# Router logits of the first twelve batches on VectorE instead of TensorE, in a fused four-layer attention and MoE kernel

## The chip, the cores and the metric

One Trainium2 chip; the kernel runs on one core of it. The metric is device microseconds for one launch, from the core's first to its last instruction and what the runtime adds around it.

## The reference

Sixteen batches of 256 tokens of width 256, float32. Four residual layers follow each other, and the last is a routed mixture of experts:

```python
x = x + L0_xattn(ctx_1024, layernorm(x))      # 8 heads of 128, keys: 256 context + 256 own rows
x = x + L0_ffn(layernorm(x))                  # 256 -> 1024 -> 256, weights changed per batch by 16 tokens
x = x + L1_xattn(layernorm(x), ctx, ctx)      # one head of width 256
x = x + L1_ffn(layernorm(x))
# L1_ffn: E = 8 experts of width 256
inh = sigmoid(x @ Wr / temperature)           # the logits: x is (256, 256) a batch, Wr is (256, 8)
w = ...                                       # weights from |inh - 1/e|, a zone, a fallback to the best two
out = sum_e w[:, e] * ((silu(x @ Wg[e]) * (x @ Wu[e])) @ Wd[e])
```

The change touches how `x @ Wr` is computed, when its results are used, and the code for rows beyond the usual capacity.

## The kernel before

The work is a stream of 128 heads (16 batches of 8) of the first attention. The outer loop `for n in range(NS + 2)` writes out one head after another: scores `sc` and their maxima `nm` (`s1`), the exponentials on ScalarE, scaling of the rows on GpSimd (`s1_scale`), 32 by 32 transposes on VectorE and a hop through DRAM to finish the transposition (`s2`, `s2_fetch`: `tb`, `hop`, `pT`), and two heads later the product with the values (`s3`: `po`, `outT`). `s0q` and `s0k` project the next head's queries and keys; their results `qT` and `kT` are moved by ScalarE or VectorE (`evict`).

Between these steps `gap` gives TensorE other work. It holds a list of jobs, generators that write out some instructions and then yield how long, in planned TensorE time (`Clock.pe`), they want to wait. The order of every engine's queue is thereby fixed when the program is built; each engine runs its queue in order and waits on semaphores. One job per batch is `chain`, everything after the first attention: the output projection `px`, the first feed-forward layer (`W1e`, `ph`, `gelu`, `W2e`, `pf`), the second attention (`pv1`, `pq1`, `sc1`, `po1`), and the logits. A second job, `route`, waits until the chain is done and turns logits into weights and slots; then GpSimd scatters the batch's rows with 16 indirect DMAs into `slots_d` (line 811), from where the experts read them. Chain b starts when head 2 of batch b + 1 is written. Jobs talk through sets: `A.fed` (the first layer of the feed-forward is written), `A.fed_forward`, `A.weighed` (the routing has read the logits).

The logits of a batch, before: the normalized rows `row` (lines 613 to 615) are transposed in 32 by 32 blocks by VectorE (`to_blocks`, line 306, tile `yd_b`), written to DRAM and fetched back as `ydT` (`from_blocks`, line 317; five DMAs on SyncE's queue), copied into order (lines 918 and 922), and multiplied by `Wr_sb` on TensorE (`pl`, four products of 128 by 8 each, eight passes). This holds for batches 0 to 13 (`hopped`); batches 14 and 15 transpose on TensorE (`turned_tile`, tile `ydT_p`).

Tiles shared in turn matter here: `W1e` holds the batch's changed first-layer weights (8 KB a partition), `pT1` the second attention's probabilities. `ev` is a row set broadcast to all partitions from DRAM (line 410), 512 KB an issue; `behind_fetch` is a list of such issues, one of which is put out per head, behind the fetch of `pT`.

The experts (`experts`, class `G`) start from head 124 on, and run on after the last head; each group of up to 512 rows is loaded, transposed through DRAM (`hop_rows_b`, `yTd`) and multiplied (`pg`, `pu`, `pd`); its results are added into the output by indirect DMAs of GpSimd (line 1324). Rows beyond the planned capacity are worked in units (class `U`); those beyond `AMONG` lie behind a branch that the device takes only if a count on the device asks for it.

Of the kernel before, what the change touches and what calls it, by code (L numbers as in the profile page):

```python
# [12 lines left out]
F32 = mybir.dt.float32  # L13
# [3 lines left out]
ALU = mybir.AluOpType  # L17
# [12 lines left out]
def xattn_ffn_kernel(  # L30
# [220 lines left out]
    WvT = keep.tile([P, DC, D], F32, name="WvT")  # L251
    Wr_sb = keep.tile([P, DC, E], F32, name="Wr_sb")

# [93 lines left out]
    def chain(b, A, behind):  # L347
# [16 lines left out]
        def raw_tile(tag, name):  # L364
            return wk.tile([P, QP, DC, TC, QB], F32, tag=tag, name=name)
# [65 lines left out]
        while behind is not None and b - 1 not in A.fed_forward:  # L431
            yield 0.4


        od = wk.tile([P, DC, 2 * NI], F32, tag="od", name=f"od_{b}")
        nc.vector.tensor_scalar(
# [84 lines left out]

        rs = ln_rstd(mv, "q")
        yield queued - 0.3
        while behind is not None and not behind.done:
            yield 0.4
        y = wk.tile([P, TC, D], F32, tag="y", name=f"yc_{b}")
        ln_apply(y, x_b, mv, rs)
# [54 lines left out]
        if hopped:  # L582
            hop = to_blocks(wk, pr, TC, "tbc", 2, f"pr1_{b}_b")
            yield SENT
            raw = raw_tile("raw_c", f"pr1T_{b}")
            from_blocks(raw, hop)
            yield LANDED + 3.0
            pT = wk.tile([P, TC, S], F32, tag="pT1", bufs=1, name=f"pT1_{b}")
            for m in range(TC):
                evict(pT[:, m, :], in_order(raw)[:, m], None, None)  # L590
            yield 4.0
        else:
            pT = turned_tile(pr, "pT1", f"pT1_{b}")
            yield 2.5
        mv = mv_tile("d")
        for c in range(TC):
            ri = small.tile([P, 1], F32, tag="ri1", name=f"ri1_{b}_{c}")
            nc.vector.reciprocal(ri, sums[c])
            po = mm_tile(D, f"po1_{b}_{c}")
            for m in range(TC):  # L600
                mm(po, pT[:, m, ts(c, P)], v1[:, m, :], start=(m == 0), stop=(m == TC - 1))
            nc.vector.scalar_tensor_tensor(
                x_b[:, c, :], po, ri, x_b[:, c, :], ALU.mult, ALU.add
            )
            stats(c, "d", mv)


        rs = ln_rstd(mv, "d")
# [4 lines left out]
        row = A.row[b] = wk.tile([P, TC, ROW], F32, tag="row", bufs=2, name=f"row_{b}")  # L613
        ln_apply(row[:, :, 0:D], x_b, mv, rs)
        nc.vector.tensor_copy(row[:, :, D + E], number[:, b * TC : (b + 1) * TC])
        if hopped:
            hop = to_blocks(wk, row, TC, "tbc", 2, f"yd_{b}_b")
            yield SENT
            raw = raw_tile("raw_c", f"ydT_{b}")
            from_blocks(raw, hop)  # L620
            yield LANDED
            ydT = wk.tile([P, DC, S], F32, tag="q1T", name=f"ydT_{b}")
            for d in range(DC):
                evict(ydT[:, d, :], in_order(raw)[:, d], None, None)
            yield 4.0
        else:
            yield 1.4
            ydT = turned_tile(row, "q1T", f"ydT_{b}")
            yield 1.6
        while b >= 1 and b - 1 not in A.weighed:  # L630
            yield 0.4
        pl = mm_tile(TC * E, f"pl_{b}")
        for c in range(TC):
            for d in range(DC):
                mm(
                    pl[:, ts(c, E)], ydT[:, d, ts(c, P)], Wr_sb[:, d, :],
                    start=(d == 0), stop=(d == DC - 1),
                )
        A.z[b] = wk.tile([P, TC, E], F32, tag="z", name=f"z_{b}")
        nc.vector.tensor_scalar(  # L640
            A.z[b].rearrange("p t e -> p (t e)"), pl, lasting["invt"], None, ALU.mult
        )


    class Plan:
# [177 lines left out]
    class A:  # L823
        xs, ctxT, outT, cin, kvT, v = {}, {}, {}, {}, {}, {}
        row, z = {}, {}
        projected, fed, fed_forward, weighed = set(), set(), set(), set()
        tails = {}


# [1 line left out]
    with ExitStack() as sh, ExitStack() as sa, ExitStack() as sf:  # L831
# [290 lines left out]
        def load_late(h):  # L1122
            if h == 0:
                nats["W2"] = load_turn(W2, DC, HC, "W2e")
            if h == 1:
                nats["Wv"] = load_turn(Wv_w, DC, DC, "v1")
                nats["qk"] = load_fold()
            if h == 5:
                nc.sync.dma_start(Wo_sb, Wo.rearrange("(h p) d -> p h d", p=P))
                nc.sync.dma_start(Wr_sb, Wr.rearrange("(c p) e -> p c e", p=P))  # L1130
                lasting["b2"] = row_everywhere(b2, "b2_bc")
                lasting["bv1"] = row_everywhere(Wv_b, "bv1_bc")
                lasting["scale"] = row_everywhere(ffn_scale, "scale_bc")
                lasting["invt"] = row_everywhere(temperature, "temp_bc")
            if h == 7:
                nc.vector.reciprocal(lasting["invt"], lasting["invt"])

        def all_turns():
# [206 lines left out]
        class U:  # L1345


            def __init__(self, part, j):
                self.part, self.j = part, j
                self.u = sum(UNITS[:part]) + j  # L1350
                self.name = f"{part}_u{j}"

            def place(self):
                return nc.values_load(
                    Plan.starts[0:1, self.u : self.u + 1], engines=(mybir.EngineType.SP,),
                    min_val=0, max_val=E * NTOKS[self.part] - P,
                )

            def expert(self):
                return nc.values_load(  # L1360
                    Plan.who[0:1, self.u : self.u + 1], engines=(mybir.EngineType.PE,),
                    min_val=0, max_val=E - 1,
                )

            def weight(self, to):
                by = D_.more.tile([P, E], F32, tag="by_u", bufs=2, name=f"by_{self.name}")
                nc.vector.tensor_tensor(by, self.rows[:, D : D + E], Plan.weigh[:, self.u], ALU.mult)
                nc.vector.tensor_reduce(to, by, AX.X, ALU.add)

            def load(self):  # L1370
                tag = ("y", "yT")[self.u % 2]
                rows = wk.tile(
                    [P, ROW], F32, tag=tag, bufs=1, name=f"rows_{self.name}",
                    padded_shape=[P, DC * S],
                )
                self.rows = rows
                nc.sync.dma_start(rows, slots_d[self.part][bass.ds(self.place(), P), :])
# [37 lines left out]
            def down(self):  # L1415
# [188 lines left out]
        some = nc.values_load(beyond[0:1, 0:1], min_val=0, max_val=1)  # L1604
        all_slots = nc.values_load(beyond[0:1, 1:2], min_val=0, max_val=1)
        with tc.If(some > 0):
            for part in range(2):
                for j in range(AMONG[part], UNITS[part]):
                    u = U(part, j)
                    u.load()  # L1610
                    u.turn()
                    u.gates()
                    u.turn_h()
                    u.down()

            with tc.If(all_slots > 0):
                for part in range(2):
# [48 lines left out]
```

## Time and profile before

| | |
|---|---|
| median of 3 runs | 1810.41 us (1808.53 to 1811.94) |
| the profiled execution's own time | 1815.16 us, its span 1813.4 us |
| TensorE (PE) busy | 1780.6 us, 98% |
| VectorE (DVE) busy | 1196.6 us, 66% |
| ScalarE (ACT) busy | 586.0 us, 32% |
| GpSimd (POOL) busy | 830.9 us, 46% |
| DMA | 325.01 MB, 179 GB/s on average |
| granted TensorE clock | 0.995 |

How to read it: a line of a group gives source line, engine, operation, the tiles written and read, the shape, the count, then the busy time, the mean duration of one, and the idle time of the engine just before, with what ended it. A line of a timeline gives the start in us from the span's start, the duration, the engine and the instruction; in brackets the engine's idle time ahead of it and what ended that. Matmuls are pipelined, so their durations overlap, and the distance between starts is what one costs. L80 is the helper that issues every matmul; tiles tell them apart. SPq is SyncE's DMA queue.

### The profile page before, as it was taken

To read this page: it belongs to the slowest core of one execution; us is meant where nothing else is said; L and a number is where in the kernel's file an instruction comes from. 1 tells how busy PE (TensorE), PEld (TensorE's weight loads), DVE (VectorE), ACT (ScalarE), POOL (GpSimd) and SP (SyncE) were. 2 spreads that over 40 slices of the span, in tenths; PEclk is the share of its full clock that TensorE was granted. 3 is DMA by queue.
4 is the path that set the end of the run, shared out by engine and by line. 5 is a ranking of instruction groups with operands and counts; after the bars stand their busy time and mean duration, and the time that the engine had idled before them with its cause. 6 is when DMAs were issued, how large, how long until landed. Compare 5 with 4: busy or idle time off the path is not lost.

```text
span 1813.4 us, 22509 instructions
## 1 busy us (share of the span) xinstructions
PE 1780.6 (98%) x6508; PEld 1206.7 (67%) x6508; DVE 1196.6 (66%) x3332; ACT 586.0 (32%) x1306; POOL 830.9 (46%) x979
## 2 busy tenths in 40 slices
PE   8999999999999999999999999999999999999987
PEld 4566666666666666666666666666666677666655
DVE  4465676767676767676767676767666667675544
ACT  3433434343434343333333333333333311211100
POOL 2122224444435353535353535353534357776765
PEclk9999999999999999999999999999999999999999
DMA  6653546565655555555556555555545668899986
GB/s 215 184 185 117 174 139 190 167 189 168 187 169 188 168 184 172 184 172 178 173 181 174 180 177 177 179 178 175 181 156 157 197 161 216 227 234 235 200 168 112
DMA packets 264746, 325.01 MB, mean 179 GB/s; under 512 B 32893, under 2 KB 217385, under 8 KB 264617
## 3 DMA queue, kind: packets, MB, share of 16 engines
q1 hardware_dynamic: 235720, 273.67, 49.9%
q0 software_dynamic: 28848, 49.83, 11.7%
q8 instruction: 54, 0.88, 0.2%
q14 instruction: 76, 0.61, 0.1%
q10 hardware_dynamic: 48, 0.01, 0.0%
HBM read 161.91 MB, written 161.48 MB: 178 GB/s over the span
## 4 chain that ended last, share of the span: by engine, by line
PE 92%; DMA 2%; DVE 2%; SPq 1%; issue 1%; POOL 1%; ACT 0%; POOLq 0%; DVEq 0%; ACTq 0%
PE po L80 13%; PE sc L80 13%; PE pv L80 13%; PE pk L80 11%; PE pq L80 7%; PE px L80 6%; PE ph L80 6%; PE pf L80 6%; PE pg L80 5%; PE pu L80 5%; PE pd L80 5%; DMA yTd<-hop_rows_b 1%; PE pl L80 1%; SPq L317 1%; DMA pT<-hop 0%
## 5 line engine op out<-in xcount | busy, mean ns | idle before, releaser
L987 ACT ACTIVATE pr<-sc,nm 128x512 f32<-128x512 f32 x256 | 173.7, 683 | 479.7 <-DVE nm L981 418.4
L995 POOL TENSOR_SCALAR pr<-pr,ri 128x512 f32<-128x512 f32 x256 | 179.0, 709 | 322.7 <-DVE ri L994 317.8
L811 POOL DMA_INDIRECT slots_d<-row,at_slot x256 | 253.2, 989 | 70.4 <-issue 70.4
L80 PE MATMUL po<-pT,v 128*128 128x256 f32 x1024 | 242.3, 379 | 2.6 <-DVE W2T L1048 1.5
L80 PE MATMUL sc<-kT,qT 128*128 128x512 f32 x512 | 241.0, 593 | 1.5 <-ACT kT L920 1.5
L80 PE MATMUL pk<-kvT,Wk_sb 128*128 128x512 f32 x512 | 241.3, 594 | 0.0
L80 PEld LDWEIGHTS po<-pT,v 128*128 128x128 f32 x1024 | 193.8, 190 | 70.8 <-issue 38.1
L80 PE MATMUL pv<-Wv_sb,kvT 128*128 128x512 f32 x512 | 235.0, 592 | 0.0
L1033 DVE TENSOR_SCALAR outT<-po,cvec 128x256 f32<-128x256 f32 x128 | 61.2, 478 | 246.0 <-PE po L80 230.1
L1003 DVE STREAM_TRANSPOSE tb<-pr 128x512 f32<-128x512 f32 x256 | 165.9, 686 | 13.2 <-DMA hop<-tb 11.7
L80 PEld LDWEIGHTS pv<-Wv_sb,kvT 128*128 128x128 f32 x512 | 97.0, 190 | 108.2 <-issue 103.1
L981 DVE TENSOR_REDUCE nm<-sc 128x1 f32<-128x512 f32 x256 | 160.3, 663 | 2.0 <-PE sc L80 1.9
L80 PEld LDWEIGHTS sc<-kT,qT 128*128 128x128 f32 x512 | 96.9, 190 | 69.9 <-issue 61.2
L80 PEld LDWEIGHTS pk<-kvT,Wk_sb 128*128 128x128 f32 x512 | 97.7, 191 | 68.4 <-issue 61.6
L80 PE MATMUL pq<-kvT,Wq_sb 128*128 128x256 f32 x512 | 133.5, 383 | 0.0
L80 PEld LDWEIGHTS pq<-kvT,Wq_sb 128*128 128x128 f32 x512 | 96.7, 191 | 41.8 <-issue 28.2
L80 PE MATMUL px<-Wo_sb,outT 128*128 128x256 f32 x512 | 121.8, 381 | 0.0
L80 PE MATMUL ph<-ybT,W1e 128*128 128x256 f32 x512 | 121.0, 379 | 0.0
L1324 POOL DMA_INDIRECT out_dram<-o,at x65 | 102.3, 1574 | 36.3 <-issue 19.2
L452 POOL TENSOR_TENSOR W2e<-ev,od 128x256 f32<-128x256 f32 x120 | 78.5, 681 | 88.0 <-DMA ev<-ev_d 88.0
L918 ACT COPY v<-pv 128x512 f32<-128x512 f32 (+1 forms) x132 | 70.8, 536 | 148.1 <-PE pv L80 146.7
L80 PE MATMUL pf<-W2e,hT 128*128 128x256 f32 x512 | 118.0, 379 | 0.0
(259 smaller groups left out, 2695.4 us busy)
## 6 DMA issues: line engine op xcount, KB each, us to landing
hop<-tb SPq DMA_DIRECT2D x128, 512.0 KB
pT<-hop SPq DMA_DIRECT2D x512, 128.0 KB
ev<-ev_d SPq DMA_DIRECT2D x32, 512.0 KB
rows<-slots_d SPq DMA_DIRECT2D x14, 530.0 KB
hop_rows_b<-rows_b SPq DMA_DIRECT2D x13, 512.0 KB
yTd<-hop_rows_b SPq DMA_DIRECT2D x52, 128.0 KB
rows<-slots_d SPq DMA_DIRECT2D x15, 397.5 KB
hop_rows_b<-rows_b SPq DMA_DIRECT2D x14, 384.0 KB
```

Source lines behind the costliest of these rows:

```text
L80: nc.tensor.matmul(out, lhsT, rhs, **kw)
L317: nc.sync.dma_start(dst[ts(m, QB)].rearrange("r a d c s -> r a (d c s)"), from_[m])
L452: (nc.gpsimd if b < B - 1 else nc.vector).tensor_tensor(W2e[:, c, d, :].rearrange("p (i a) -> p i a", i=NI), evs[1][:, :, c * NA : (c + 1) ...
L811: ins = nc.gpsimd.indirect_dma_start(out=slots_d[part], out_offset=bass.IndirectOffsetOnAxis(ap=at_slot[:, c, e : e + 1], axis=0), in_=row ...
L918: nc.scalar.copy(out, src)
L981: nc.vector.tensor_reduce(nm, sc, AX.X, ALU.max, negate=True)
L987: nc.scalar.activation(pr, sc, AF.Exp, bias=nm, accum_out=sm)
L995: nc.gpsimd.tensor_scalar(pr, pr, ri, 1.0, ALU.mult, ALU.mult)
L1003: nc.vector.transpose(tb[:, :, c, :], heads[n][c][0].rearrange("p (m f) -> p m f", m=QP))
L1033: nc.vector.tensor_scalar(o, po, col("bv", h), None, ALU.add)
L1324: ins = nc.gpsimd.indirect_dma_start(out=out_rows[0 : sum(NTOKS[: self.part + 1]), :], out_offset=bass.IndirectOffsetOnAxis(ap=self.at[:, ...
```

## The change

For batches 0 to 11 the logits are computed on VectorE. `Wr` is transposed once at the start and stored in DRAM (`WrT_d`). For each such batch two DMAs broadcast it to all partitions, four experts each (512 KB), into the tile `W1e`, after the next batch's `ph` is written; then 16 `tensor_tensor_reduce` operations, one for each expert and each 128 rows, multiply a row tile by one expert's vector and sum along the row. They are spaced by 1.4 of planned time. The transposes, the hop and the products `pl` of these batches are gone. Batches 12 to 15 take the path of TensorE's transposes, which before only 14 and 15 took.

The waits between jobs follow: the next chain's `W1e` waits until the logits two batches back are written (`A.scored`), its use of `pT1` until those one batch back are, and its second attention waits for the previous second attention (`A.attended`) rather than the whole previous chain. Routing of a batch still waits for its chain and so comes later.

The units of the first part that lie behind the branch become a loop on the device (class `W`).

```diff
@@ -251,6 +251,10 @@
     WvT = keep.tile([P, DC, D], F32, name="WvT")
     Wr_sb = keep.tile([P, DC, E], F32, name="Wr_sb")
+    WrT_d = dram.tile([E, D], F32, tag="WrT_d", bufs=1, name="WrT_d")
+    zero = keep.tile([P, 1], F32, name="zero")
+    nc.gpsimd.memset(zero, 0.0)
+
@@ -429,6 +433,9 @@
             yield 0.2
         yield max(landed[0], there) - Clock.pe
         while behind is not None and b - 1 not in A.fed_forward:
+            yield 0.4
+
+        while b >= 2 and b - 2 not in A.scored:
             yield 0.4
@@ -521,7 +528,7 @@
         rs = ln_rstd(mv, "q")
         yield queued - 0.3
-        while behind is not None and not behind.done:
+        while behind is not None and b - 1 not in A.attended:
             yield 0.4
         y = wk.tile([P, TC, D], F32, tag="y", name=f"yc_{b}")
         ln_apply(y, x_b, mv, rs)
@@ -585,6 +592,8 @@
             raw = raw_tile("raw_c", f"pr1T_{b}")
             from_blocks(raw, hop)
             yield LANDED + 3.0
+            while behind is not None and b - 1 not in A.scored:
+                yield 0.4
             pT = wk.tile([P, TC, S], F32, tag="pT1", bufs=1, name=f"pT1_{b}")
             for m in range(TC):
                 evict(pT[:, m, :], in_order(raw)[:, m], None, None)
@@ -603,6 +612,7 @@
                 x_b[:, c, :], po, ri, x_b[:, c, :], ALU.mult, ALU.add
             )
             stats(c, "d", mv)
+        A.attended.add(b)
         rs = ln_rstd(mv, "d")
@@ -613,33 +623,60 @@
         row = A.row[b] = wk.tile([P, TC, ROW], F32, tag="row", bufs=2, name=f"row_{b}")
         ln_apply(row[:, :, 0:D], x_b, mv, rs)
         nc.vector.tensor_copy(row[:, :, D + E], number[:, b * TC : (b + 1) * TC])
-        if hopped:
-            hop = to_blocks(wk, row, TC, "tbc", 2, f"yd_{b}_b")
-            yield SENT
-            raw = raw_tile("raw_c", f"ydT_{b}")
-            from_blocks(raw, hop)
-            yield LANDED
-            ydT = wk.tile([P, DC, S], F32, tag="q1T", name=f"ydT_{b}")
-            for d in range(DC):
-                evict(ydT[:, d, :], in_order(raw)[:, d], None, None)
-            yield 4.0
+        if b < B - 4:
+
+
+            while b + 1 not in A.fed:
+                yield 0.4
+
+            yield 12.0
+            Wr_all = wk.tile([P, E, D], F32, tag="W1e", name=f"Wr_all_{b}")
+            landed = []
+
+            def wr_everywhere(half):
+                nc.sync.dma_start(
+                    Wr_all[:, ts(half, E // 2), :].rearrange("p e d -> p (e d)"),
+                    WrT_d[ts(half, E // 2)].rearrange("e d -> (e d)").partition_broadcast(P),
+                )
+                landed.append(Clock.pe + 8.0)
+
+            behind_fetch.extend([lambda: wr_everywhere(0), lambda: wr_everywhere(1)])
+            while b >= 1 and b - 1 not in A.weighed:
+                yield 0.4
+            z = A.z[b] = wk.tile([P, TC, E], F32, tag="z", name=f"z_{b}")
+            part_of = wk.tile([P, D], F32, tag="pT1", name=f"zy_{b}", padded_shape=[P, TC * S])
+            for e in range(E):
+                if e % (E // 2) == 0:
+                    half = e // (E // 2)
+                    while len(landed) <= half:
+                        yield 0.2
+                    yield landed[half] - Clock.pe
+                for c in range(TC):
+                    nc.vector.tensor_tensor_reduce(
+                        out=part_of, in0=row[:, c, 0:D], in1=Wr_all[:, e, :], op0=ALU.mult,
+                        op1=ALU.add, scale=1.0, scalar=zero, accum_out=z[:, c, e : e + 1],
+                    )
+                    yield 1.4
+            z = z.rearrange("p t e -> p (t e)")
+            nc.vector.tensor_scalar(z, z, lasting["invt"], None, ALU.mult)
         else:
             yield 1.4
             ydT = turned_tile(row, "q1T", f"ydT_{b}")
             yield 1.6
-        while b >= 1 and b - 1 not in A.weighed:
-            yield 0.4
-        pl = mm_tile(TC * E, f"pl_{b}")
-        for c in range(TC):
-            for d in range(DC):
-                mm(
-                    pl[:, ts(c, E)], ydT[:, d, ts(c, P)], Wr_sb[:, d, :],
-                    start=(d == 0), stop=(d == DC - 1),
-                )
-        A.z[b] = wk.tile([P, TC, E], F32, tag="z", name=f"z_{b}")
-        nc.vector.tensor_scalar(
-            A.z[b].rearrange("p t e -> p (t e)"), pl, lasting["invt"], None, ALU.mult
-        )
+            while b >= 1 and b - 1 not in A.weighed:
+                yield 0.4
+            pl = mm_tile(TC * E, f"pl_{b}")
+            for c in range(TC):
+                for d in range(DC):
+                    mm(
+                        pl[:, ts(c, E)], ydT[:, d, ts(c, P)], Wr_sb[:, d, :],
+                        start=(d == 0), stop=(d == DC - 1),
+                    )
+            A.z[b] = wk.tile([P, TC, E], F32, tag="z", name=f"z_{b}")
+            nc.vector.tensor_scalar(
+                A.z[b].rearrange("p t e -> p (t e)"), pl, lasting["invt"], None, ALU.mult
+            )
+        A.scored.add(b)
     class Plan:
@@ -823,7 +860,8 @@
     class A:
         xs, ctxT, outT, cin, kvT, v = {}, {}, {}, {}, {}, {}
         row, z = {}, {}
-        projected, fed, fed_forward, weighed = set(), set(), set(), set()
+        projected, fed, fed_forward, attended = set(), set(), set(), set()
+        scored, weighed = set(), set()
         tails = {}
@@ -1133,6 +1171,14 @@
                 lasting["scale"] = row_everywhere(ffn_scale, "scale_bc")
                 lasting["invt"] = row_everywhere(temperature, "temp_bc")
             if h == 7:
+                tp = tr_tile("WrT_p")
+                for d in range(DC):
+                    turned(tp[0:E, d, :], Wr_sb[:, d, :], ident)
+                WrT = wk.tile(
+                    [E, D], F32, tag="pT1", bufs=1, name="WrT", padded_shape=[E, TC * S]
+                )
+                nc.vector.tensor_copy(WrT, tp[0:E, 0:DC, :].rearrange("p d s -> p (d s)"))
+                nc.sync.dma_start(WrT_d, WrT)
                 nc.vector.reciprocal(lasting["invt"], lasting["invt"])
         def all_turns():
@@ -1347,30 +1393,34 @@
             def __init__(self, part, j):
                 self.part, self.j = part, j
-                self.u = sum(UNITS[:part]) + j
+                u = self.u = sum(UNITS[:part]) + j
+                self.of = slice(u, u + 1)
+                self.tag = ("y", "yT")[u % 2]
                 self.name = f"{part}_u{j}"
             def place(self):
...
@@ -1429,11 +1479,21 @@
                 )
                 apart(ins, f"out_{self.name}", others(self.part))
+        class W(U):
+
+
+            def __init__(self, j):
+                self.part, self.u = 0, j
+                self.name = "0_w"
+                self.of = bass.ds(j, 1)
+
+            tag = "y"
+
         class V(U):
             def __init__(self, part, e, t, j):
-                self.part, self.u = part, j
+                self.part, self.tag = part, ("y", "yT")[j]
                 self.e, self.t = e, t
                 self.name = f"{part}_v{j}"
@@ -1604,14 +1664,13 @@
         some = nc.values_load(beyond[0:1, 0:1], min_val=0, max_val=1)
         all_slots = nc.values_load(beyond[0:1, 1:2], min_val=0, max_val=1)
         with tc.If(some > 0):
-            for part in range(2):
-                for j in range(AMONG[part], UNITS[part]):
-                    u = U(part, j)
-                    u.load()
-                    u.turn()
-                    u.gates()
-                    u.turn_h()
-                    u.down()
+            with tc.For_i(AMONG[0], UNITS[0]) as j:
+                u = W(j)
+                u.load()
+                u.turn()
+                u.gates()
+                u.turn_h()
+                u.down()
             with tc.If(all_slots > 0):
                 for part in range(2):
```

More of the change, by code (lines that the diff above doesn't have):

```diff
@@ L1354, in place @@
                 return nc.values_load(
-                    Plan.starts[0:1, self.u : self.u + 1], engines=(mybir.EngineType.SP,),
+                    Plan.starts[0:1, self.of], engines=(mybir.EngineType.SP,),
                     min_val=0, max_val=E * NTOKS[self.part] - P,
@@ L1360, in expert @@
                 return nc.values_load(
-                    Plan.who[0:1, self.u : self.u + 1], engines=(mybir.EngineType.PE,),
+                    Plan.who[0:1, self.of], engines=(mybir.EngineType.PE,),
                     min_val=0, max_val=E - 1,
@@ L1366, in weight @@
                 by = D_.more.tile([P, E], F32, tag="by_u", bufs=2, name=f"by_{self.name}")
-                nc.vector.tensor_tensor(by, self.rows[:, D : D + E], Plan.weigh[:, self.u], ALU.mult)
+                nc.vector.tensor_tensor(
+                    by, self.rows[:, D : D + E],
+                    Plan.weigh[:, self.of].rearrange("p u e -> p (u e)"), ALU.mult,
+                )
                 nc.vector.tensor_reduce(to, by, AX.X, ALU.add)
             def load(self):
-                tag = ("y", "yT")[self.u % 2]
                 rows = wk.tile(
-                    [P, ROW], F32, tag=tag, bufs=1, name=f"rows_{self.name}",
+                    [P, ROW], F32, tag=self.tag, bufs=1, name=f"rows_{self.name}",
                     padded_shape=[P, DC * S],
```

## The prediction

> **What bounds the kernel now.** I read the page first (shares of each engine), then the table of stretches, then what TensorE (PE) waits for, and last the order of time around the operations that the change removes.
>
> From the page and from the stretches (length, busy time of PE, PEld, DVE, ACT, POOL, granted clock, DMA share, GB/s):
>
> ```profile
> PE 1780.6 (98%) x6508; PEld 1206.7 (67%) x6508; DVE 1196.6 (66%) x3332; ACT 586.0 (32%) x1306; POOL 830.9 (46%) x979
> ...
> 340.00:1330.00 990.00, 989.16 (x3615) 675.91 (x3614) 693.98 (x1944) 363.05 (x822) 443.91 (x576) 1.00 0.57 177
> ...
> 1600.00:1700.00 100.00, 99.05 (x345) 64.32 (x344) 60.47 (x162) 16.42 (x33) 66.93 (x49) 1.00 0.97 246
> ```
>
> In the steady part PE is idle 0.84 us of 990. Two equal pieces of the chain of waits (pf at 902.94 and 993.82) give a batch of 90.9 us, so that stretch is 10.9 batches, and VectorE (DVE) works 693.98 / 10.9 = 63.7 us of each: 27 us are free. The time is PE's sum; another engine counts only where it makes PE wait. In the last 300 us the DMA engines are nearly full as well.
>
> PE's own waits, total, times and longest:
>
> ```profile
> PE pg L80 <- DMA yTd<-hop_rows_b: 5.9, 4, 2.8
> PE pl L80 <- ACT ydT L918: 1.9, 1, 1.9
> ```
>
> The second is the wait of batch 13 for the very hop that the change removes.
>
> **The change part by part.**
>
> *Logits leave PE (12 batches).* PE in order of time, batch 5:
>
> ```profile
> 715.06 0.95 PE L80 MATMUL pl<-Wr_sb,ydT 128*128 128x8 f32 x8
> 715.87 1.11 PE L80 MATMUL pq<-kvT,Wq_sb 128*128 128x256 f32 x4
> 716.82 1.89 PE L80 MATMUL pf<-W2e,hT 128*128 128x256 f32 x8
> ```
>
> Durations overlap in the pipe; starts count: pl holds PE 715.87 - 715.06 = 0.81 us. 12 x 0.81 = 9.7 us leave a queue that has no gap.
>
> *Batches 12 and 13 turn their rows on PE.* They keep pl and, no longer hopping, get four transposes each. The trace has this for batch 14:
>
> ```profile
> 1481.18 0.60 PE L84 MATMUL ydT_p<-ident,row 128*128 128x128 f32 x4
> 1481.62 1.89 PE L80 MATMUL pd<-wx,hTd 128*128 128x256 f32 x8
> ```
>
> 0.44 us each, 0.9 for two; the two small transposes of Wr at the start, at the same pitch, 0.2. Net PE work: -9.7 + 0.9 + 0.2 = -8.6 us. Batches 14 and 15 in the trace wait for no row there; in the changed order batch 12 has about 8 us of other PE work between po1 and its transposes, batch 13 about 4, against 2.9 us for the way through DVE (0.48 + 0.43 + 0.18), POOL (0.23 + 0.72) and DVE (0.74) with hand-overs. Bounds 0 to 3 us in all; I take 1.0, because DVE carries more there.
>
> *Batch 13's wait goes.* Around it:
>
> ```profile
> 1437.48 1.14 PE L80 MATMUL pl<-Wr_sb,ydT 128*128 128x8 f32 x8 [1.94 <-ACT ydT L918]
> ...
> 1438.84 2.94 PE L80 MATMUL pg<-yTd,wx 128*128 128x512 f32 x4
> 1441.57 2.56 PE L80 MATMUL pu<-yTd,wx 128*128 128x512 f32 x4
> 1443.97 1.89 PE L80 MATMUL pf<-W2e,hT 128*128 128x256 f32 x8
> ```
>
> Idle 1.94 us, and then pg and pu take 2.73 and 2.40 from start to start where the same form takes 1.72 elsewhere: 1.7 us more, with a granted clock of 0.83 over 1435 to 1445. The rule (Trainium skill, "TensorE: Matmul & The Clock Gate", Part 1) is that PE falls to half clock after an idle window of about 3.4 us; by it a gap of 1.94 us would cost 1.94 alone. The row decides: the gap cost 3.6, and the gaps of 2.8 and 2.58 us at 1743 and 1760 are followed by pg of 3.57 and 3.54 likewise. So any stall of 2 us counts nearly double, removed or new; gaps of 0.3 to 0.5 us (865 and 1047) left no slow matmul. The changed order of PE puts other work there (batch 14's pf, px and attention stand later among the experts), so something else may be late in its place: bounds 0 to -3.6; I take half, -1.8.
>
> *DVE takes the logits.* Groups of DVE (count | busy, mean ns | idle before):
>
> ```profile
> L553 DVE CUSTOM_DVE_ANT_0 pr<-yc,g,g 128x256 f32<-128x256 f32 x32 | 15.0, 507 | 0.0
> L553 DVE DVE_READ_ACCUMULATOR2_ANT rc<- 128x1 f32 x32 | 2.7, 85 | 0.0
> L306 DVE STREAM_TRANSPOSE yd_b<-row 128x256 f32<-128x256 f32 x28 | 10.6, 414 | 0.0
> L922 DVE COPY ydT<-ydT 128x256 f32<-128x256 f32 x26 | 16.9, 689 | 0.0
> ```
>
> The same multiply-and-sum on the same shape exists: 0.507 + 0.085 = 0.59 us. Sixteen a batch are 9.5 us; two transposes (0.83) and two copies (1.38) go: +7.3 us a batch, 63.7 to 71.0 of 90.9, or 78%. Over 12 batches 87 us of DVE, beside PE, hidden by the 27 us free per batch.
>
> Where they stand: in the built programs' order they lie in four heads of the next batch (3, 7, 3 and 3 of them), which hold the two lightest DVE stretches (5.8 of 8 us and 3.4 of 8 us at 659 and 667) and one of the heaviest (8.0 of 9 at 634); what is queued behind each is the next heads' transposes and row maxima. The tightest head is the first: its kT ends on ACT at 640.97 + 0.72 = 641.69, and the sc that needs it starts at 642.31: 0.62 us of slack. There the operations stand behind the row maxima, while the routing arithmetic that stood ahead of them (2.0 us) moves two heads on and the input's normalization and transposes (1.6 us) come in: roughly even. Hidden, then; bounds 0 to 0.6 us a batch.
>
> A rule against the change is in "SBUF — State Buffer", section "SBUF: two separate sides": a DVE operation with two SBUF operands and a GpSimd operation that reads SBUF hold one port pair in turn, and the later blocks entirely. The trace shows such pairs: rows' normalization takes 740 ns (row<-x) against 403 (yc<-x), each time beside POOL's scaling of pr, and W2e's add 1150 ns at 707 against 670. By the existing row alone DVE gains 7.3 us a batch; by the rule every operation that meets POOL (4.8 of 11 us busy) waits some 0.35 us more, 16 x 0.43 x 0.35 = 2.4 us, so 9.7 us a batch and 81%. Both leave PE's sum alone; I take the row, with the rule's figure in the range.
>
> *Broadcasts and queues.* Per batch SP drops five issues (hop_yd_b, four ydT: 0.34 + 1.74 us) and gains two of 512 KB, of the kind of ev<-ev_d (0.43 each). ev was issued at 696.54 and used by POOL at 701.75, so it lands in 5.2 us; the order gives Wr_all 8. It waits for W1e's last reader, a batch's phase earlier, and only the multiplies wait for it. If late, DVE stands still with later maxima behind it; the DMA share of 0.57 makes that unlikely. The traffic grows by half a megabyte of some 16 per batch. Planner waits (on scored, attended) leave px, W1e, ph, po1 of batches 0 to 12 in the same heads as before. Cost 0, as long as those 2.8 us of margin hold.
>
> *POOL's scatters move.* POOL, same head:
>
> ```profile
> L811 POOL DMA_INDIRECT slots_d<-row,at_slot x256 | 253.2, 989 | 70.4 <-issue 70.4
> ...
> 701.75 2.32 POOL L452 TENSOR_TENSOR W2e<-ev,od 128x256 f32<-128x256 f32 x4 [6.52 <-DMA ev<-ev_d]
> ...
> 710.63 1.23 POOL L452 TENSOR_TENSOR W2e<-ev,od 128x256 f32<-128x256 f32 x2
> ```
>
> Routing runs half a batch later, so the 16 scatters (0.989 + 0.275 = 1.26 us each) come among the W2e products: two before them (inside the 6.5 us wait), four between, six behind. Four add 5.1 us; POOL's idle stretches of 1.92 and 0.70 us there absorb about 2.6, so the last product ends about 2.5 us later, 714.4, and its add on DVE at 715.1. pf's second half, which needs it, now follows sc directly, at 715.06, and reads the last block in its second half, 715.9. It fits by 0.8 us. Bounds 0 and 1.0 us a batch; I take 0.05, 0.6 us in all.
>
> *The loop behind the branch, the zero tile, WrT:* code that is not run (the page's operations show only three units) and single small instructions; 0, cover for the latter being the first batch's PE work.
>
> **Sum.** -8.6 + 1.0 - 1.8 + 0.6 = -8.8 us. Against the profiled execution's own time: 1815.16 - 8.8 = 1806.4. That execution lies 4.75 us above the median of the runs; carried to the median, 1810.41 - 8.8 = 1801.6 us.
>
> **Rivals.**
>
> 1. *POOL's queue decides (slower).* If the scatters push the last W2e product beyond the 0.8 us margin, PE stalls in each of 11 or 12 batches at pf. 1.55 us later than I estimate cancels the gain (0.75 x 12 = 9); at 3 us later the stall is 2.2 x 12 = 26, less 8.8: 1810.4 + 17 = about 1828 without the clock's share. For: POOL's queue is strict, and 10 of 16 scatters lie in that head. Against: POOL sat waiting 6.5 us for ev, and that transfer no longer stands behind hop_yd_b. Chance 0.17.
> 2. *The gain is lost in the tail (same).* From 1480 on DMA is 0.9 or more busy; if it, not PE, sets the pace, 8.8 us become longer waits at pg for yTd (already 2.8 and 2.6 us). Time 1809 to 1812. Against: those transfers are issued by the progress of PE's own groups, so they shift with it, and the order of PE is the same as before from batch 15's ph on. Chance 0.12.
> 3. *DVE is late in the tight head.* 0.3 us past its slack is 3.6 us: 1805. Chance 0.08, still faster.
>
> The forecast itself: 0.63, with its own range 1797 to 1806.
>
> **How the numbers follow.** 0.2% is 3.6 us, about what a measurement of this kernel tells from no change. Faster: 0.63 + 0.08 = 0.71; same 0.12; slower 0.17. The range runs from 1796.5 (all of batch 13's stall back, no new wait: -8.6 - 3.6, and run spread) to 1812 (the tail's case), leaving out most of rival 1.
>
> **What would show it.** Right: pl counts 32 instead of 128 records; the steady stretch shortens by 0.8 us a batch with PE still without gaps; DVE's share 77 to 81% there. Wrong: waits of PE pf on DVE W2e (rival 1), of PE sc on ACT kT (rival 3), of DVE on Wr_all's DMA, or longer waits at pg after 1700 (rival 2).

## The result: slower, by about 17.6 us

The changed kernel takes 1827.09 us (median of 4 runs, 1825.32 to 1831.08) where the kernel before takes 1809.47 (4 runs); the ratio is 1.0096, 95% interval 1.0083 to 1.0109. Forecast were 1801.6 and a gain. The profiled execution has a span of 1823.5 us (1825.32 in its own time), against 1813.4 (1815.16) before. The two spans differ by 10.1 us and the medians by 17.6, since the profiled execution of before lies 5.7 us above its median and that of the changed kernel 1.8 below. So the parts below are told from the traces, and their sum is held against the medians.

From the page of the changed kernel and from its stretches (length, busy time of PE, PEld, DVE, ACT, POOL, granted clock, DMA share, GB/s):

```profile
PE 1777.7 (97%) x6422; PEld 1197.7 (66%) x6423; DVE 1273.9 (70%) x3661; ACT 587.7 (32%) x1308; POOL 858.6 (47%) x980
...
340.00:1330.00 990.00, 980.11 (x3505) 662.05 (x3504) 765.18 (x2233) 361.14 (x817) 465.02 (x574) 1.00 0.58 183
...
1600.00:1700.00 100.00, 99.09 (x346) 64.62 (x346) 64.87 (x202) 15.29 (x30) 66.16 (x49) 1.00 0.94 236
```

In the steady stretch PE was idle for 0.84 us of 990 before; now it is idle for 9.9. DVE rose from 693.98 to 765.18 us there, or to 77%. That rise was forecast. What costs the time is read from PE's own waits (total, times, longest):

```profile
PE pf L80 <- DVE W2e L467: 6.8, 12, 1.8
...
PE pg L80 <- DMA yTd<-hop_rows_b: 5.2, 4, 2.3
PE ydT_p L84 <- DVE row L286: 4.8, 3, 2.2
PE pq L80 <- DMA ycT<-hop_yc_b: 4.7, 4, 2.4
PE sc L80 <- DVE kT L962: 2.1, 1, 2.1
PE po L80 <- DMA pT<-hop: 2.1, 2, 1.8
```

Three of these are new and come more than once: pf (eleven batches, and once more later), pq (four batches) and ydT_p (batches 12 and 13). The last two lines, at sc and at po, are new as well, with one wait each of about 2 us after the steady part. The wait that was in the tail before, pg for yTd, is no longer than it was.

Where the time went, by the starts of PE's operations in order of time (head 16 is the first sc of batch 2, head 112 that of batch 14, head 120 that of batch 15; yT_u is the first unit; differences of starts, in us):

| kernel | heads 16 to 112 | PE idle in it | head 120 to yT_u | yT_u to PE's last | after it |
|---|---|---|---|---|---|
| before | 1091.4 | 1.1 | 325.2 | 124.7 | 12.5 |
| changed | 1094.7 | 9.4 | 340.1 | 120.4 | 8.8 |

So it is no slow tail. Between heads 16 and 112 stand eleven of the twelve pl that leave PE, so 8.9 us (11 x 0.81) were to be won there, and 3.3 are lost. Another 14.9 us are lost in the stretch in which batches 12 to 14 run beside the first experts. The end is 8 us shorter.

**The new wait at pf.** Three views of the same microseconds, POOL, then DVE, then PE (start, length, idle time before it and what ended it):

```profile
709.28 0.23 POOL L280 TENSOR_SCALAR rs_c<-mv_c 128x2 f32<-128x2 f32 x1 [1.73 <-DVE mv_c L274]
709.59 0.72 POOL L281 TENSOR_TENSOR rs_c<-rs_c,mhalf 128x2 f32<-128x2 f32 x1
710.50 1.48 POOL L848 DMA_INDIRECT slots_d<-row,at_slot  x1 [0.19 <-issue]
712.29 0.97 POOL L848 DMA_INDIRECT slots_d<-row,at_slot  x1 [0.30 <-issue]
713.28 1.18 POOL L459 TENSOR_TENSOR W2e<-ev,od 128x256 f32<-128x256 f32 x2
```

```profile
714.50 0.69 DVE L467 TENSOR_TENSOR W2e<-W2e,W2T 128x512 f32<-128x512 f32 x1 [2.89 <-POOL W2e L459]
```

```profile
713.79 1.03 PE L80 MATMUL pf<-W2e,hT 128*128 128x256 f32 x4
715.25 1.13 PE L80 MATMUL pf<-W2e,hT 128*128 128x256 f32 x4 [0.43 <-DVE W2e L467]
716.22 1.03 PE L80 MATMUL pq<-kvT,Wq_sb 128*128 128x256 f32 x4
```

Two scatters stand right ahead of the last product of W2e. DVE waits 2.89 us for that product, and PE stops in the middle of pf's second half, at the block that the product feeds. It repeats in eleven batches, with 0.42 to 0.61 us of idle time each; in starts, pf takes 7.3 us more in heads 16 to 112 than before (90.2 for 82.9).

**The new wait at pq.** SP's queue in the changed kernel while the heads of batch 8 run (the ycT is that of batch 6):

```profile
732.04 3.29 SPq L1054 DMA_DIRECT2D pT<-hop  x4
735.38 0.42 SPq L637 DMA_DIRECT2D Wr_all<-WrT_d  x1
735.90 1.83 SPq L321 DMA_DIRECT2D raw<-hop_cn  x4
...
738.86 3.88 SPq L321 DMA_DIRECT2D ycT<-hop_yc_b  x4
```

The same two groups of issues before:

```profile
731.91 1.81 SPq L1016 DMA_DIRECT2D pT<-hop  x4
...
737.32 2.26 SPq L317 DMA_DIRECT2D ycT<-hop_yc_b  x4
```

PE in the changed kernel:

```profile
745.47 3.02 PE L80 MATMUL pq<-ycT,M 128*128 128x256 f32 x8 [2.38 <-DMA ycT<-hop_yc_b]
748.28 2.56 PE L80 MATMUL po<-pT,v 128*128 128x256 f32 x8
```

The four issues of ycT take 3.88 us in place of 2.26, and SP comes to them late, behind pT (3.29 us for four in place of 1.81) and a broadcast. Over batches 1 to 12 the four issues take 3.33 us in the mean, 2.31 before. PE waits 2.38 us, and then pq and po take 2.81 and 2.40 from start to start where 1.73 is usual: another 1.7 us.

**The new waits in batches 12 and 13.** DVE just before the first row that PE now turns, and PE:

```profile
1433.34 1.29 DVE L1041 STREAM_TRANSPOSE tb<-pr 128x512 f32<-128x512 f32 x2
1434.55 1.25 DVE L1019 TENSOR_REDUCE nm<-sc 128x1 f32<-128x512 f32 x2
1435.72 0.86 DVE L483 TENSOR_SCALAR hT<-ph,cvec 128x256 f32<-128x256 f32 x2
1436.49 0.87 DVE L451 SCALAR_TENSOR_TENSOR W1e<-ev,od,W1T 128x256 f32<-128x256 f32 x2
1437.28 0.22 DVE L1032 RECIPROCAL ri<-sm 128x1 f32<-128x1 f32 x2
1437.42 1.11 DVE L286 TENSOR_SCALAR row<-x,mv_d,rs_d 128x256 f32<-128x256 f32 x2
```

```profile
1437.87 0.33 PE L84 MATMUL ydT_p<-ident,row 128*128 128x128 f32 x1 [2.22 <-DVE row L286]
1438.58 0.55 PE L84 MATMUL ydT_p<-ident,row 128*128 128x128 f32 x3 [0.38 <-DVE row L286]
1439.80 1.88 PE L80 MATMUL pl<-Wr_sb,ydT 128*128 128x8 f32 x8 [0.68 <-ACT ydT L373]
1441.53 3.76 PE L80 MATMUL ph<-ybT,W1e 128*128 128x256 f32 x8
```

The row's statistics were done at 1433.4, and POOL had rs_d ready at 1434.55; until 1437.4 other work stands ahead of the normalization in DVE's queue. PE waits 3.3 us in three pieces, and ph after it takes 3.55 us from start to start in place of 1.73; the granted clock of 1435 to 1450 is 0.77. Batch 13 loses 2.24 us at 1510.95. There POOL has rs_d ready only at 1509.0, behind two scatters of slots and one of output, and DVE's other work holds the normalization until 1510.5. Between the two, pf waits 1.77 us for W2e at 1472.44.

### The profile page after: what moved, and what is told of

Read it like the earlier page. It is cut to its first block, busy times and chain, and to the rows that moved or that the text cites. A ratio compares the mean times of both kernels' runs of the same rounds, so it can differ in the third digit from the quotient of the medians.

```text
span 1823.5 us, 22575 instructions
## 1 busy us (share of the span) xinstructions
PE 1777.7 (97%) x6422; PEld 1197.7 (66%) x6423; DVE 1273.9 (70%) x3661; ACT 587.7 (32%) x1308; POOL 858.6 (47%) x980
## 5 line engine op out<-in xcount | busy, mean ns | idle before, releaser
L1033 POOL TENSOR_SCALAR pr<-pr,ri 128x512 f32<-128x512 f32 x256 | 190.9, 755 | 315.9 <-DVE ri L1032 312.3
L848 POOL DMA_INDIRECT slots_d<-row,at_slot x256 | 266.6, 1041 | 103.5 <-issue 62.5
L80 PE MATMUL pf<-W2e,hT 128*128 128x256 f32 x512 | 123.0, 381 | 6.8 <-DVE W2e L467 6.8
L80 PEld LDWEIGHTS pf<-W2e,hT 128*128 128x128 f32 x512 | 96.3, 190 | 36.2 <-issue 12.9
L80 PE MATMUL px<-Wo_sb,outT 128*128 128x256 f32 x512 | 118.0, 379 | 0.0
```

The source lines that it names most:

```text
L80: nc.tensor.matmul(out, lhsT, rhs, **kw)
L848: ins = nc.gpsimd.indirect_dma_start(out=slots_d[part], out_offset=bass.IndirectOffsetOnAxis(ap=at_slot[:, c, e : e + 1], axis=0), in_=row ...
L1033: nc.gpsimd.tensor_scalar(pr, pr, ri, 1.0, ALU.mult, ALU.mult)
```

## The experiments

Times are medians; "before" is that of the same chip's runs (1809.47 for the first four, 1808.68 for e5 to e8, 1811.21 for e9 to e12). The stretches (heads 16 to 112, and head 120 to yT_u) are worked out as in the table above.

### e1: batches 12 and 13 as before

```
         if b < B - 4:
             ...
+        elif hopped:                # batches 12 and 13: hop, ydT, pl, as before
+            hop = to_blocks(wk, row, TC, "tbc", 2, f"yd_{b}_b")
+            ...
         else:
```

> Batches 12 and 13 get their logits as before (rows hopped through the DMA engines, product pl on TensorE); batches 0 to 11 keep VectorE's logits. From the first pf of batch 14 on, TensorE's order is then that of the kernel before. Theory T (three places of loss: each batch's pf waits 0.43 us for W2e behind two scatters, some batches' pq waits for ycT behind the broadcasts, and the rearranged stretch of batches 12 to 14): the first two stay (about 0.54 x 11 = 6 and 4.7 of idle time with slow matmuls behind it, 6), the third goes: -9.7 + 0.2 + 6 + 6 = 2.5 us above before, so 1812 where before is 1809.5, and 15 us below the changed kernel. Rival R (the loss is the load as such: VectorE at 70% and the broadcasts, all along the run): within 3 us of the changed kernel, about 1825.

1814.18 us, ratio 1.0018 (1.0003 to 1.0033): 12.9 us below the changed kernel. The stretch from head 120 to yT_u falls from 340.1 to 327.6; heads 16 to 112 keep their loss (1093.3, PE idle 9.5). So the turn of the rows of batches 12 and 13 on PE costs some 12.5 us in the changed kernel, and load as such is not the cause.

### e2 and e5: everything but the logits, and the loop alone

```
-        if b < B - 4:               # e2: VectorE's logits in no batch
+        if b < 0:
```

> All logits on TensorE as before; the rest of the change stays (the waits on scored and attended, the zero tile, the turned copy of Wr, the loop behind the branch). TensorE's order is that of before but for the two small transposes of Wr. Theory T: as before plus 0.2 us, within 2 us of it. Rival W (the waits on scored or attended, the new code behind the branch, or the place of tiles cost something by themselves): 3 us or more above before.

```
-            for part in range(2):   # e5: the kernel before with this hunk and its classes only
-                for j in range(AMONG[part], UNITS[part]):
+            with tc.For_i(AMONG[0], UNITS[0]) as j:
```

> The kernel before, with only the loop behind the branch (the branch isn't taken; the code behind it is shorter). Logits on TensorE with all that was around them. Theory L (the 4 us that e2_logits_pe is faster than before come with the loop): 1805 to 1806 where before is 1809.5. Rival (they come from the other parts that e2_logits_pe keeps: waits, places of tiles, turned Wr): as before, within 1.5 us of 1809.5.

e2: 1805.57 us, ratio 0.9978 (0.9965 to 0.9991); its steady part is that of before (1090.8). The waits on scored and attended cost nothing here, where the logits come as early as before. It is faster than before, which no theory had; e5 was run for that: 1806.79 us, 0.9988 (0.9978 to 0.9997), 1.9 us faster. The intervals overlap, so the loop has about half of e2's gain or all of it; the other parts of e2 weren't split. The end of the program shows where it sits. Last scatter of the output and the page's span, of before, then of e5:

```profile
1802.60 1.54 POOL L1324 DMA_INDIRECT out_dram<-o_more,at  x1 [0.30 <-issue]
...
span 1813.4 us, 22509 instructions
```

```profile
1798.30 1.54 POOL L1324 DMA_INDIRECT out_dram<-o_more,at  x1 [0.30 <-issue]
...
span 1806.2 us, 22506 instructions
```

From the end of that scatter to the end of the span are 9.2 us before and 6.4 in e5. The code behind the branch is jumped over in both and is longer in the first. The other traces with the loop agree: 6.9 us in e2, 5.2 to 5.4 in the changed kernel and in all the other runs.

### e3: no scatter among W2e's products

```
+        A.making = True
         for c in range(NI):
             w2_block(c)
             ...
+        A.making = False
 ...
             for e in range(E):
+                while A.making and b < B - 4:
+                    yield 0.4
                 ins = nc.gpsimd.indirect_dma_start(
```

> The changed kernel, but no scatter of a row's slots is issued between the first and the last W2e product of the chain that runs beside it (four scatters fewer there, the same number later). Theory T: W2e's last product ends 2.7 us or more sooner, pf waits for it in no steady batch, and a batch of the steady part shrinks from 90.75 to about 90.2 us; 11 x 0.54 = 6 us less, 1821 where the changed kernel has 1827 (less if the end gives part of it back). Rival (pf waits for the addition on VectorE, which is late by VectorE's own queue and not by POOL's): pf's wait stays at about 0.43 and the time within 2 us of 1827.

1810.69 us, ratio 1.0006 (0.9991 to 1.0021): 16.4 us below the changed kernel, more than expected. POOL and PE at the same place:

```profile
705.98 1.63 POOL L459 TENSOR_TENSOR W2e<-ev,od 128x256 f32<-128x256 f32 x2
707.78 1.52 POOL L852 DMA_INDIRECT slots_d<-row,at_slot  x1 [0.17 <-issue]
```

```profile
708.64 1.88 PE L80 MATMUL sc<-kT,qT 128*128 128x512 f32 x4
710.36 1.89 PE L80 MATMUL pf<-W2e,hT 128*128 128x256 f32 x8
712.09 1.03 PE L80 MATMUL pq<-kvT,Wq_sb 128*128 128x256 f32 x4
```

The product now ends 1.0 us before its batch's sc (708.64), where it ended 2.4 us after it in the changed kernel (712.07 and 714.46): 3.4 us sooner. pf's second half runs in one piece. Heads 16 to 112 take 1083.4 us, 11.3 less. By the differences of starts pf has 7.3 of them (82.9 us, as before), or some 0.7 a batch (0.43 idle, the rest around it), and the waits for ycT (4.7 to 2.8 us in all) with the slow matmuls behind them have the rest. Why pq waited less here is not settled, since ycT has the same time to arrive in both (PE reaches pq 12.55 us after yc_b is ready where it doesn't wait).

### e4: both edits

> Both edits: batches 12 and 13 by TensorE as before, and no scatter between the first and the last W2e product. Theory T: 1812 - 6 = 1806, 3 to 4 us faster than before; what is left of the 9.7 us is lost at pq behind the broadcasts. Rival R (load as such): 1820 or more.

1805.08 us, ratio 0.9971 (0.9957 to 0.9985), as expected: 4.4 us faster than before. Heads 16 to 112 take 1082.2, but head 120 to yT_u takes 332.1, 7 us more than before: batch 13's pl waits 4.5 us, which is more than the 1.94 of before. Against e3 the hop of batches 12 and 13 is worth 7.2 us in that stretch (339.3 to 332.1) and 5.6 in the medians, not the 12.5 of e1: with the scatters moved, something else disturbs the stretch (see e11).

### e6 and e7: the broadcasts, doubled and on another queue

```
+                for _ in range(2):          # e6, on top of e3
                     nc.sync.dma_start(Wr_all[...], WrT_d[...].partition_broadcast(P))
```

> e3_gate, with each broadcast of Wr issued twice (four transfers of 512 KB a batch in place of two; the second writes the same values). Theory D (pq waits for ycT because the broadcasts stand ahead of ycT's way): pq waits in most of the 12 batches, 1 to 3 us each, with slow matmuls behind: 12 us or more above e3_gate, 1822 and more. Rival S (the slack of ycT shrank by pl's 0.8 us and what waits there is chance): within 2 us of e3_gate, 1811.

```
-                nc.sync.dma_start(          # e7, on top of e3
+                nc.scalar.dma_start(
                     Wr_all[...], WrT_d[...].partition_broadcast(P))
```

> e3_gate, with the broadcasts of Wr issued by ScalarE instead of SP: they no longer stand in the queue that ycT's transfers go through, but use the same DMA engines and carry the same bytes. Theory Q (the order of SP's queue delays ycT): pq's waits (2.8 us in e3_gate) vanish, 3 to 4 us less, 1807. Rival (the engines' time is what they share): pq's waits stay, within 2 us of 1810.7; or ScalarE, held by its issue until W1e is free, is late with kT or pr, and the time grows.

e6: 1896.42 us, ratio 1.0476 (1.0458 to 1.0493): 86 us more than e3. PE's wait, and SP at one such place:

```profile
PE pq L80 <- DMA ycT<-hop_yc_b: 58.4, 12, 6.0
```

```profile
763.90 5.48 SPq L640 DMA_DIRECT2D Wr_all<-WrT_d  x2
769.42 1.88 SPq L321 DMA_DIRECT2D raw<-hop_cn  x4
...
772.30 3.26 SPq L321 DMA_DIRECT2D ycT<-hop_yc_b  x4
```

The second of the two broadcasts, issued twice, takes SP 5.48 us, and ycT stands behind it. PE's idle time at pq is 58.4 us, 55.6 more than in e3; the rest goes with slow matmuls after the waits (mean granted clock 0.979 in place of 0.993).

e7: 1807.69 us, ratio 0.9989 (0.998 to 0.9998), 3 us below e3. The bytes are the same, the queue is not:

```profile
732.91 2.26 SPq L321 DMA_DIRECT2D ycT<-hop_yc_b  x4
```

```profile
PE pq L80 <- DMA ycT<-hop_yc_b: 0.9, 2, 0.7
```

ycT's four issues take 2.26 us again, and pq waits 0.9 us in all. Heads 16 to 112 take 1081.1 us: against 1090.5 and 1090.8 in e5 and e2 that is 9.6 less. The eleven pl in it have 8.9 of that, so their gain is there in full; the rest is small differences at other products.

### e9: the other queue, with the scatters left where they are

> The changed kernel with one edit: the broadcasts of Wr are issued by ScalarE in place of SP. The scatters stay among the W2e products. Theory (three separate losses): pq's waits and the slow matmuls behind them go, 5 to 7 us; pf's waits (0.43 us idle, 0.69 us in starts, 11 batches) and the stretch of batches 12 to 14 stay: 1820 to 1822. Rival (ycT is late because pf was late, so pq's waits follow pf's): within 2 us of 1827.

1817.86 us, ratio 1.004 (1.0026 to 1.0053), 10 us below the changed kernel by the ratios:

```profile
PE pf L80 <- DVE W2e L467: 6.8, 12, 1.8
...
PE pq L80 <- DMA ycT<-hop_yc_b: 0.5, 1, 0.5
```

pq's waits go although pf's stay. So the losses are separate. Heads 16 to 112: changed 1094.7, e9 1087.5, e7 1081.1. The queue is worth 7.2 us and the scatters 6.4.

What was late is the issuing and not the transfer. Where PE waits for ycT in the changed kernel, it starts 2.5 to 3.2 us after the end of the last of the four issues; in e7 and e9, where it still waits at three places, 3.1 to 3.2 us after. But the four issues take 3.33 us in the mean over batches 1 to 12 of the changed kernel, and 2.64 and 2.63 in e7 and e9.

### e8, e10, e11 and e12: the stretch of batches 12 to 14

```
             for d in range(DC):             # e8, on top of e4
                 evict(ydT[:, d, :], in_order(raw)[:, d], None, None)
-            yield 4.0
+            yield 8.0
```

> e4_hop_gate, with 8 instead of 4 us planned between the copies of ydT and its product pl in batches 12 and 13, so that TensorE has other work in front of it. Theory: the wait of 4.5 us at pl in batch 13 and the 1.6 us of slow matmuls behind it go, 4 to 6 us less: 1800, 9 us faster than before. Rival (what comes next is held by the DMA engines, so it is only moved to the waits at pg and ydT_p after 1560): 1803 to 1806, as e4_hop_gate.

```
-                nc.sync.dma_start(          # e10, on top of e4
+                nc.scalar.dma_start(
 ...
-        if b < B - 4:                       # e11: B - 5, e12: B - 6
+        if b < B - 5:
```

> e4_hop_gate with the broadcasts issued by ScalarE: no scatters among the products, batches 12 and 13 as before, pq without waits. Theory: the 1.5 us of idle time left at pq and the slow matmuls behind it go, 1803; the 9.7 us of pl are had up to batch 14, and half of it is given back in the stretch of batches 12 to 14 (pl in batch 13, 4.5 us). Rival: the ends are held by the DMA engines, within 1 us of 1805.

> As e10_hop_gate_act, but VectorE takes the logits of batches 0 to 10 only; batches 11 to 13 by TensorE as before. Theory (the stretch of batches 12 to 14 is late because the logits and scatters of batch 11, half a batch later than before, lie in it): TensorE's wait at pl in batch 13 falls from 4.5 to about 2 us as before, and the stretch from head 120 to the first unit's yT_u takes 326 us as before in place of 332: -0.9 x 11 - 2 = 12 us below before, 1798. Rival (the end is held by transfers): 1803 or more, with waits of more than 6 us at pg for yTd.

> As e11_to_10, with batches 0 to 9 only. Theory: the stretch is as before already with 11 batches, so one batch less costs 0.9 us: 1799. If the stretch is still disturbed by batch 10, this one is faster than e11_to_10.

e8: 1810.36 us, ratio 1.0006 (0.9997 to 1.0014), 6 us more than e4 by the ratios: the rival's way, and further than it had it. The wait at pl went, and a larger one came behind it:

```profile
PE pg L80 <- DVE yTd L988: 7.7, 2, 5.9
```

e10: 1801.86 us, ratio 0.9947 (0.9934 to 0.9961). Its stretch is that of e4 (331.8). e11: 1794.98 us, ratio 0.9913 (0.99 to 0.9927). This is the fastest of all, 16 us faster than before where its sum had 12. Batch 13's wait in e10, then in e11:

```profile
PE pl L80 <- ACT ydT L984: 4.2, 1, 4.2
```

```profile
PE pl L80 <- ACT ydT L984: 1.3, 1, 1.3
```

Its stretch takes 325.5 us as before, and heads 16 to 112 take 1080.1. e12: 1798.1 us, ratio 0.9933 (0.992 to 0.9947): the stretch is 324.3, so little more is won there, and a batch of pl comes back; the 3.1 us that it is slower than e11 are more than the 0.9 expected for that, and the intervals overlap. What disturbs the stretch in e4 and e10 is thus batch 11's logits half a batch later. Whether its 16 products on DVE or its scatters on POOL do it was not tried; e1, which has both (its scatters unhindered), takes only 327.6 there, at a point where PE is 13 us later.

## Why the prediction was wrong, by its own steps

The sign was wrong because three terms of the sum were far too small: the scatters (0.6), the broadcasts (0) and the turned rows of batches 12 and 13 (1.9 with their own work). They measured 6.4, 7.2 and 12.5 us, against a gain from pl that came as forecast. Rival 1 named the wait at pf, and its 1828 us is close to the measured 1827.09. That is luck: its wait gave 6.4 of the loss, and the rest came at pq and in batches 12 and 13, which it did not name.

- **PE without pl (-9.7): right.** Heads 16 to 112, with eleven of the twelve, take 1081.1 and 1080.1 us in e7 and e11 for 1090.6: 9.5 and 10.5 less, where 8.9 are due.
- **DVE takes the logits, hidden: right.** 71.2 us more in the steady 990 are 6.5 a batch (10.9 batches); by the existing row 7.3 were expected, by the rule on the shared port pair 9.7. The measurement is on the row's side. The new operation takes 569 ns in the mean where 507 was read: 470 where no POOL operation ran beside it (84 of 192), 733 where one did for more than nine tenths of its time (36). So it does take longer beside POOL's work, by 0.26 us where 0.35 were set for the rule. No sc waited for kT in the steady part.
- **POOL's scatters move (taken at +0.6, bound 1.0 a batch): mis-sized; they cost 6.4 us in heads 16 to 112 (e9 against e7).** The number and place of the scatters were right: two, four, six. That the idle stretches of 1.92 and 0.70 us absorb 2.6 us was wrong: the last two scatters stand directly ahead of the last product, behind rs_c, and no idle stretch lies there. They take 2.97 us (710.31 to 713.28). The second error: the need was read in the time of before (715.9), but PE had gained 1.27 us by then, so it came at 714.82, and the add that was put at 715.1 ended at 715.19. What a step saves upstream comes off the margin downstream. Rival 1 priced this wait at 0.75 and 2.2 us a batch; it is about 0.7 at pf.
- **The broadcasts (taken at 0): wrong; 7.2 us (the changed kernel against e9).** The step asked whether Wr_all lands in time for DVE, and it does (0.6 us of idle time in all). It did not ask what is queued behind it: ycT. From yc_b ready to pq, ycT had 13.4 us before; it has 12.55 now that PE comes there sooner, and in the place shown above it took 15.1. The Trainium skill ("DMA: Bandwidth & Descriptors", section "Issuing engines are not separate DMA queues") says that starting transfers on several engines only saves the time to initiate them, usually little. Here that time was the loss: the same bytes by ScalarE's queue gave back 7.2 us in the changed kernel.
- **Batches 12 and 13 turn their rows on PE (taken at 0.9 + 1.0, bound 3): mis-sized; about 12.5 us (the changed kernel against e1).** The way of the row was costed as a chain of durations with hand-overs (2.9 us), and "about 8 us of other PE work" was set against it. In batch 12 that way took 6.3 us (1432.26 to 1438.53) and in batch 13 7.2 (1504.05 to 1511.23): what stood ahead of the row in DVE's queue, and in batch 13 in POOL's as well, wasn't counted. Nor were there 8 us of PE work between in batch 12, but 4: po1 ended at 1431.61, and PE came to the transposes at 1435.65. The prediction itself said that a stall of 2 us counts nearly double, and after both of these the granted clock fell to 0.50, for 6.8 and 3.4 us. Beside moved scatters (e3 against e4) the term is 7.2 us and not 12.5.
- **Batch 13's wait goes (-1.8): it went, and nothing was won.** Its pl at 1514.82 waits for nothing, but its row's turn, ahead of it, waits 2.24 us. In the runs that keep the hop the wait is there again, 1.3 (e11) to 4.5 us (e4); e8 alone moved it elsewhere.
- **The loop (taken at 0): a gain of 1.9 us (0.5 to 4.0 by the interval of e5),** at the end of the program. The Trainium skill ("Runtime: NRT & Kernel Launch", section "Instruction fetch mechanics") has a taken branch wait for its target's code when that lies outside what was fetched. The 9.2 and 6.4 us could come from that, but no run shows that it is the fetch.
- **The tail as the bound (rival 2): no.** From yT_u to PE's last the changed kernel takes 120.4 us for 124.7. (The prediction's DMA share of "0.9 or more" from 1480 on was read too high: it was 0.88 to 1600, 0.97 to 1700 and 0.74 after that.)

The sum of the sizes as measured: -9.6 + 6.4 + 7.2 (heads 16 to 112) + 14.9 (the stretch, its transposes included) - 1.9 (the loop) = +17.0, against 17.6 in the medians. This is an account and no independent proof. The first three are differences along one row of traces (e2 and e5, e7, e9, the changed kernel), so they add up to what that part lost by construction; and the end, 8.0 us shorter in the one pair of traces, stands in the sum only with the loop's 1.9 from the medians.

## What to carry to other kernels

When an operation leaves the bound engine, everything that was timed against it is needed earlier by what it saved: take the saving off each margin before saying that something still fits. For each thing that is moved or added to a queue, list what stands behind it there, in POOL's and SP's queue as well as in DVE's; here three small insertions ahead of a tight operand cost some 26 us between them, each measured with at least one other in place, and the intended gain was there all the time. Work that is hidden in the steady part may not be in the last batches: stop the change a few batches before the stages change, as e11 does.

## What was not expected of the hardware

- SP's issues stretch with what was issued before them: the four issues of ycT took 3.33 us in the mean (2.71 to 4.25) with two 512 KB broadcasts a batch in SP's queue, and 2.63 (2.18 to 3.03) with them in ScalarE's (e9). Two such broadcasts in a row took SP 5.48 us in e6.
- A stall of PE of about 2 us can be followed by matmuls at half speed, and need not be. In the changed kernel the stalls of 2.38 us (745), 2.22 (1438, with 0.38 and 0.68 close behind) and 2.24 us (1511) were followed by a granted clock of 0.50 for 3.4, 6.8 and 3.4 us, and pq, po and ph took 2.81, 2.40 and 3.55 us for 1.73 each. After stalls of 2.10 us (1362) and 2.33 (1761) the clock stayed at 1.00. In e6, 58 us of idle time at pq come with a loss of 86. What decides was not tried.
- Code behind a branch that is never entered can cost time at the end of the program: 9.2 us from the last scatter to the end of the span with four unrolled units behind the branch, 5.2 to 6.9 in all the traces with a loop. In the medians e5, which has the loop alone, gains 1.9 us (0.5 to 4.0). One trace of the unrolled form is all there is.
